# Attention transposes in a graph kernel: 128x128 transposes on TensorE replaced by 32x32 block transposes on VectorE and a round trip through DRAM

## The chip, the cores and the metric

The kernel runs on one core of one Trainium2 chip. Its time is the device time of one execution in microseconds (us). The kernel before takes 3298.03 us, the median of three runs between 3296.64 and 3298.12 us. The engines are called as in the profile: PE is TensorE (PEld its weight loads), DVE VectorE, ACT ScalarE, POOL GpSimd; SP is the engine whose queue issues all the DMAs of this kernel.

## The reference

There are 128 graphs of 128 nodes with 256 features each, all in float32. Three layers of graph attention are followed by a gated graph network (GRU) of three steps. Each layer works on the normalized, rectified input and adds its result to it:

```python
h = jnp.maximum(_layernorm(x, axis=-1), 0.0)
x = x + gnn(h, adj, W, a)          # three attention layers
# one attention layer, per graph
Wh = h @ W
e = leaky_relu((Wh @ a1)[:, None] + (Wh @ a2)[None, :], 0.2)
att = softmax(where(adj > 0, e, -9e15), axis=-1)
out = elu(att @ Wh)                # the third layer multiplies by a node mask before elu
# the gated layer, three steps
aggr = A.T @ (h @ weight[i])
r, z = sigmoid(..), sigmoid(..);  n = tanh(i_n + r * h_n)
h = (1 - z) * n + z * h
```

A matrix product on TensorE sums over the partitions of both operands. `h @ W` therefore needs h with its features on the partitions, and `att @ Wh` needs att with its columns on the partitions. Both lie the other way round when they are computed, node by partition, so each attention layer transposes h (two blocks of 128x128 per graph) and att (one block per graph), and the gated network needs the transpose of its first h as well.

## The kernel before

The 128 graphs are worked on in 32 groups of G = 4. For each group there are two programs. `gat(g)` (lines 276 to 295) loads x and adj, derives two masks from adj (`cap`, `am`), runs three attention layers and then the normalization for the gated network. `gru(g)` (lines 297 to 393) runs three steps of the gated network and stores the result. They are written down in the order gat(0), gat(1), gru(0), gat(2), gru(1), gat(3), and so on (lines 401 to 407). The Tile framework then orders the instructions by itself: it plays the program through ahead of time, and among the instructions whose operands it holds to be ready an engine takes the one that was written down first. The result is one fixed order per engine, and on the chip an engine that waits for an operand holds up everything behind it in its own order. So an instruction of gat(g+1) goes ahead of gru(g) and behind gru(g-1), and gru(g) fills what gat(g+1) leaves free.

A tile with a tag has as many buffers as its pool says, and the tiles of one tag take them in the order in which they are written down. The pools `gw` and `grp` have two buffers (the tags `x3` and `am` three). PSUM's eight banks are dealt out by line 62: three to attention (`gat`), four to the GRU's gates (`gru`), one to the GRU's transposes and aggregations (`tr`).

One attention layer (lines 196 to 272) goes as follows.

- `normed` (line 162): DVE takes mean and variance of each row (`st`, `mv`, lines 167 and 168), POOL turns the variance into 1/sqrt (`ve`, `rs`, lines 170 and 172), DVE writes the normalized rows `xn` (line 175).
- `relu_T` (line 181): eight PE transposes of 128x128 into two PSUM banks (`hTp`, line 187), which ACT (line 191) and DVE (line 193) rectify into `hT`.
- `whp` (line 207): PE multiplies hT by W, to which two columns W@a1 and W@a2 are appended; ACT copies each result to `wh` (line 211).
- `e` (line 216) spreads the second score along the rows with a PE transpose of a broadcast column; DVE adds the first score, applies the mask and the leaky slope and takes the row maximum (lines 222 to 228); ACT takes the exponential and its row sums (line 232); DVE inverts the sums (line 236); POOL scales the rows (`pe`, line 239) and prepares x - 1 (`xm`, line 244).
- `atp` (line 248): four PE transposes of att, which DVE copies to `at` (line 250).
- `hp` (line 256): PE multiplies at by wh; ACT and DVE compute elu and add x (lines 262 to 268), which gives the x of the next layer, `xo`.

After the third layer, `normed` and `relu_T` run a fourth time (lines 290 to 293): hT is then the first h of the GRU with features on partitions, and POOL rectifies xn into `hn`, the same with nodes on partitions. In the GRU the transposes `hnp` (line 308) turn later h back to nodes on partitions, `agp` (line 334) multiplies by the adjacency, and the gate products go through `mm` (line 317).

All DMAs are issued by SP: loads of x and adj at lines 69 and 71, the store of the result at line 392.

Of the kernel before, what the change touches and what calls it, by code (L numbers as in the profile page):

```python
# [8 lines left out]
FT = mybir.dt.float32  # L9
# [12 lines left out]
def kernel(  # L22
# [23 lines left out]

    nc = tc.nc
# [14 lines left out]
    BANKS = {"gat": 3, "gru": 4, "tr": 1}  # L62
# [95 lines left out]
    setup.close()  # L158
    rw = ctx.enter_context(tc.tile_pool(name="rw", bufs=2))


    def normed(xt, name):
# [3 lines left out]
        for b in range(G):  # L166
            nc.vector.bn_stats(st[:, b, :], xt[:, b, :])  # L167
            nc.vector.bn_aggr(mv[:, b, :], st[:, b, :])
        ve = gw.tile([P, G], FT, tag="ve", name=f"ve_{name}")
# [3 lines left out]
        xn = gw.tile([P, G, D], FT, tag="xn", name=f"xn_{name}")  # L173
        for b in range(G):
            nc.vector.tensor_scalar(  # L175
                xn[:, b, :], xt[:, b, :], mv[:, b, 0:1], rs[:, b : b + 1],
                op0=OP.subtract, op1=OP.mult,
            )
        return xn

    def relu_T(xn, pool, tag, name):

        hT = pool.tile([P, KD, T], FT, tag=tag, name=f"hT_{name}")
        for k in range(KD):
            ps = bank("gat", f"hTp_{name}_{k}")
            for b in range(G):
                nc.tensor.transpose(  # L187
                    ps[:, b * P : (b + 1) * P], xn[:, b, k * P : (k + 1) * P], ident
                )
            if k % 2 == 0:  # L190
                nc.scalar.activation(hT[:, k, :], ps, AF.Relu)  # L191
            else:
                nc.vector.tensor_scalar_max(hT[:, k, :], ps, 0.0)
        return hT

    def attention(g, l, xt, cap):

        name = f"{g}_{l}"
        xn = normed(xt, name)
        hT = relu_T(xn, gw, "hT", name)  # L200
# [3 lines left out]
        for c in range(G):  # L204
            ps = bank("gat", f"whp_{name}_{c}")
            for k in range(KD):
                nc.tensor.matmul(  # L207
                    ps[:, :E], hT[:, k, c * P : (c + 1) * P], W[l][:, k, :],
                    start=(k == 0), stop=(k == KD - 1),
                )  # L210
            nc.scalar.copy(wh[:, c, :], ps[:, :E])  # L211
# [17 lines left out]
        pe = gw.tile([P, G, N], FT, tag="pe", name=f"pe_{name}")  # L229
        sm = gw.tile([P, G], FT, tag="sm", name=f"sm_{name}")  # L230
        for b in range(G):
            nc.scalar.activation(
                pe[:, b, :], em[:, b, :], AF.Exp, bias=nmx[:, b : b + 1], accum_out=sm[:, b : b + 1]
# [3 lines left out]
        if l == 2:  # L237
            nc.vector.tensor_mul(ri, ri, nmT[:, g * G : (g + 1) * G])
        nc.gpsimd.tensor_tensor(  # L239
            pe, pe, ri.rearrange("p (g o) -> p g o", o=1).to_broadcast([P, G, N]), op=OP.mult  # L240
        )

        xm = gw.tile([P, G, D], FT, tag="xm", name=f"xm_{name}")
        nc.gpsimd.tensor_scalar(xm, xt, 1.0, -1.0, op0=OP.mult, op1=OP.add)
        yield
        atp = bank("gat", f"atp_{name}")
        for b in range(G):
            nc.tensor.transpose(atp[:, b * P : (b + 1) * P], pe[:, b, :], ident)
        at = gw.tile([P, T], FT, tag="at", name=f"at_{name}")
        nc.vector.tensor_copy(at, atp)  # L250
        xo = grp.tile([P, G, D], FT, tag=f"x{l + 1}", name=f"xo_{name}", bufs=3 if l == 2 else 2)
        for j in range(G // 2):
            hp = bank("gat", f"hp_{name}_{j}")
            for b in range(2):
                c = 2 * j + b
                nc.tensor.matmul(  # L256
                    hp[:, b * D : (b + 1) * D], at[:, c * P : (c + 1) * P], wh[:, c, :D],
# [5 lines left out]
            u = gw.tile([P, T], FT, tag="u", name=f"u_{name}_{j}")  # L263
            nc.vector.scalar_tensor_tensor(  # L264
                u, hp, 0.0, xm[:, 2 * j : 2 * j + 2, :].rearrange("p b d -> p (b d)"),
                op0=OP.max, op1=OP.add,
            )
            nc.vector.scalar_tensor_tensor(  # L268
# [174 lines left out]
```

## Time and profile before

| | before |
|---|---|
| median of three runs | 3298.03 us |
| the profiled execution: its time, its span | 3297.82 us, 3296.0 us |
| granted TensorE clock, mean | 0.992 |
| PE busy | 3089.3 us, 94% |
| DVE busy | 1889.7 us, 57% |
| ACT busy | 1076.1 us, 33% |
| POOL busy | 461.8 us, 14% |
| DMA share of 16 engines | 4.5% in the one queue that carries the kernel's own data |

The span is the time from the first to the last instruction. Busy time counts an instruction from start to end, and a matmul overlaps the next one, so a row of matmuls is better measured by the distance between their starts; the chain view gives that distance, since it lists each instruction only up to the start of what follows it. "The chain" is the sequence of work that ended last, followed back from the last instruction to whatever released it. "To landing" is the time from the issue of a DMA to the moment at which its completion is signalled. A float32 product appears as two matmul instructions.

### The profile page before, as it was taken

The page shows a single profiled execution, that of the slowest core. Times are in us where ns is not written, and L with a number is a line of the kernel's source. Part 1 is how long each engine was busy: PE and PEld are TensorE (multiplying, and loading weights), DVE is VectorE, ACT ScalarE, POOL GpSimd, SP SyncE. Part 2 cuts the span into 40 slices and gives each one's busy share as a digit, 9 for nine tenths or more (in the row PEclk, how much of TensorE's full clock was granted, in tenths as well). Part 3 has the DMA queues.
Part 4 walks back from the last instruction along what each step waited for, and adds up shares of the span by engine and source line. Part 5 has one row for each costly group of instructions (what it writes and reads, how often), then busy time and mean ns, then how long its engine had stood idle before and what let it go on. Part 6 is the DMA issues. An engine that isn't in the chain of part 4 may idle for free.

```text
span 3296.0 us, 30815 instructions
## 1 busy us (share of the span) xinstructions
PE 3089.3 (94%) x11093; PEld 1743.6 (53%) x11093; DVE 1889.7 (57%) x4216; ACT 1076.1 (33%) x2369; POOL 461.8 (14%) x486
## 2 busy tenths in 40 slices
PE   5799999999999999999999999999999999999999
PEld 3455555555555555555555555555555555555554
DVE  4555655555655555655556555556555556555553
ACT  1233333333333333333333333333333333333332
POOL 0111111111111111111111111111111111111110
PEclk8899999999999999999999999999999999999999
DMA  2000000000000000000000000000000000000000
GB/s 81 10 16 17 10 7 17 17 16 10 13 10 17 17 17 10 7 17 17 16 17 10 7 17 16 17 10 16 7 17 17 17 10 7 16 13 7 7 1 13
DMA packets 56186, 47.93 MB, mean 15 GB/s; under 512 B 3296, under 2 KB 55648, under 8 KB 56032
## 3 DMA queue, kind: packets, MB, share of 16 engines
q1 hardware_dynamic: 56032, 45.95, 4.5%
q8 instruction: 87, 1.43, 0.2%
q14 instruction: 67, 0.55, 0.1%
HBM read 29.17 MB, written 16.78 MB: 14 GB/s over the span
## 4 chain that ended last, share of the span: by engine, by line
PE 60%; DVE 22%; POOL 10%; ACT 5%; issue 2%; DMA 0%; SPq 0%; ACTq 0%; POOLq 0%; DVEq 0%
PE r L317 11%; PE whp L207 11%; PE z L317 10%; PE nn L317 6%; PE ni L317 5%; PE hTp L187 5%; POOL rs L172 4%; DVE u L264 4%; DVE xo L268 4%; DVE st L167 3%; PE agp L334 3%; POOL pe L239 3%; PE hp L256 3%; DVE xn L175 3%; PE hnp L308 2%
## 5 line engine op out<-in xcount | busy, mean ns | idle before, releaser
L317 PE MATMUL r<-ag,wc 128*128 128x512 f32 x768 | 377.8, 597 | 0.0
L317 PE MATMUL z<-ag,wc 128*128 128x512 f32 x768 | 371.0, 592 | 0.0
L207 PE MATMUL whp<-w,hT 128*128 128x258 f32 x1536 | 368.9, 389 | 0.3 <-ACT hT L191 0.2
L317 PE MATMUL ni<-ag,wc 128*128 128x512 f32 x768 | 366.1, 592 | 0.0
L239 POOL TENSOR_TENSOR pe<-pe,ri 128x512 f32<-128x512 f32 x96 | 99.9, 1040 | 1893.4 <-PE agp L334 988.9
L363 ACT ACTIVATE r<-r,brz 128x512 f32<-128x512 f32 x192 | 132.0, 687 | 602.0 <-PE r L317 602.0
L207 PEld LDWEIGHTS whp<-w,hT 128*128 128x128 f32 x1536 | 283.7, 191 | 82.0 <-ACT hT L191 16.2
L222 DVE SCALAR_TENSOR_TENSOR em<-e,wh,cap 128x128 f32<-128x128 f32 x384 | 108.1, 344 | 380.4 <-PE e L216 380.4
L358 ACT ACTIVATE wn<-nn,bh 128x512 f32<-128x512 f32 x192 | 132.0, 687 | 532.7 <-PE nn L317 532.7
L365 DVE SCALAR_TENSOR_TENSOR n<-r,wn 128x512 f32<-128x512 f32 x192 | 131.8, 687 | 303.4 <-ACT r L363 303.3
L187 PE MATMUL hTp<-ident,xn 128*128 128x128 f32 x1024 | 185.9, 292 | 107.2 <-DVE xn L175 107.2
L317 PE MATMUL nn<-h,whh 128*128 128x512 f32 x512 | 261.8, 593 | 0.0
L317 PE MATMUL z<-h,whh 128*128 128x512 f32 x512 | 261.5, 592 | 0.0
L317 PE MATMUL r<-h,whh 128*128 128x512 f32 x512 | 261.3, 592 | 0.0
L334 PEld LDWEIGHTS agp<-am,hn 128*128 128x128 f32 x1536 | 205.6, 192 | 99.1 <-issue 62.6
L317 PEld LDWEIGHTS z<-ag,wc 128*128 128x128 f32 x768 | 143.5, 190 | 168.9 <-issue 168.9
L211 ACT COPY wh<-whp 128x258 f32<-128x258 f32 x384 | 143.9, 375 | 262.2 <-PE whp L207 262.2
L317 PEld LDWEIGHTS ni<-ag,wc 128*128 128x128 f32 x768 | 143.3, 190 | 155.3 <-issue 153.6
L187 PEld LDWEIGHTS hTp<-ident,xn 128*128 128x128 f32 x1024 | 118.0, 142 | 202.8 <-PE z L317 91.4
L334 PE MATMUL agp<-am,hn 128*128 128x128 f32 x1536 | 215.6, 277 | 1.7 <-POOL hn L293 1.6
L175 DVE TENSOR_SCALAR xn<-xo,mv,rs 128x256 f32<-128x256 f32 x384 | 132.6, 408 | 142.9 <-POOL rs L172 142.9
L317 PEld LDWEIGHTS r<-ag,wc 128*128 128x128 f32 x768 | 133.1, 190 | 132.9 <-issue 91.7
(80 smaller groups left out, 4425.8 us busy)
## 6 DMA issues: line engine op xcount, KB each, us to landing
x<-in_x_dram SPq DMA_DIRECT2D x32, 512.0 KB, 3.9
out_dram<-o SPq DMA_DIRECT2D x32, 512.0 KB, 2.9
adj<-in_adj_dram SPq DMA_DIRECT2D x32, 256.0 KB, 2.7
w<-in_L_gnn_W_dram SPq DMA_DIRECT2D x3, 256.0 KB, 5.8
ab<-in_L_gnn_a_dram SPq DMA_DIRECT2D x3, 256.0 KB, 5.5
whh_ld<-in_L_gnn_w_hh_dram SPq DMA_DIRECT2D x1, 768.0 KB, 8.4
wih_ld<-in_L_gnn_w_ih_dram SPq DMA_DIRECT2D x1, 768.0 KB, 6.6
gt_ld<-in_L_gnn_weight_dram SPq DMA_DIRECT2D x3, 256.0 KB, 3.0
```

Source lines behind the costliest of these rows:

```text
L172: nc.gpsimd.tensor_tensor(rs, ve, mhalf, op=OP.pow)
L175: nc.vector.tensor_scalar(xn[:, b, :], xt[:, b, :], mv[:, b, 0:1], rs[:, b : b + 1], op0=OP.subtract, op1=OP.mult,)
L187: nc.tensor.transpose(ps[:, b * P : (b + 1) * P], xn[:, b, k * P : (k + 1) * P], ident)
L207: nc.tensor.matmul(ps[:, :E], hT[:, k, c * P : (c + 1) * P], W[l][:, k, :], start=(k == 0), stop=(k == KD - 1),)
L211: nc.scalar.copy(wh[:, c, :], ps[:, :E])
L239: nc.gpsimd.tensor_tensor(pe, pe, ri.rearrange("p (g o) -> p g o", o=1).to_broadcast([P, G, N]), op=OP.mult)
L264: nc.vector.scalar_tensor_tensor(u, hp, 0.0, xm[:, 2 * j : 2 * j + 2, :].rearrange("p b d -> p (b d)"), op0=OP.max, op1=OP.add,)
L268: nc.vector.scalar_tensor_tensor(xo[:, 2 * j : 2 * j + 2, :].rearrange("p b d -> p (b d)"), t, 1.0, u, op0=OP.min, op1=OP.add,)
L317: nc.tensor.matmul(ps, w[:, k, c * P : (c + 1) * P], v[k], start=start, stop=stop)
L334: nc.tensor.matmul(ps[:, b * P : (b + 1) * P], hn[k][b], am[:, b, :], start=True, stop=True)
L358: nc.scalar.activation(wn, nn, AF.Identity, bias=bh[:, cn : cn + 1])
L363: nc.scalar.activation(r, pr, AF.Tanh, bias=brz[:, cr : cr + 1], scale=0.5)
```

## The change

The transposes `hTp` and `atp` leave TensorE. DVE's `transpose` turns every 32x32 block of its operand in place of its own, so a 128x128 matrix comes out as a 4x4 grid of turned blocks that still stand in their old places. Moving block (q, j) to place (j, q) means moving it to other partitions. That is done by DMA: `exchange` stores the turned tile to a DRAM tile in one DMA and reads it back with four, each of which fills 32 partitions from four places in DRAM. All five are issued by SP, and the four reads wait for the store.

Around it:

- `stats` takes the place of `normed`. xn is now relu(x - mean) by ACT, without the factor rs, which is positive and is applied later, when ACT copies `whp` to `wh`. DVE negates the mean (`nm`).
- `turned` makes DVE's block transposes (two of 512 elements per partition for xn, one for att) and calls `exchange`. The elements are written interleaved by graph and feature half, so that each row in DRAM is contiguous; hT and at are therefore read by the matmuls with a step of 8 and of 4 elements between neighbouring columns, where the columns lay side by side before.
- The exponential is written over its input `em`, and the scaling by the inverted sums moves from POOL to DVE.
- POOL writes x - 1 directly into `xo`, and the elu steps work in place there; the tiles `xm`, `u` and `pe` are gone.
- For the GRU's first h, ACT computes `hn` with both mean and rs; DVE turns its two halves and each goes through its own exchange. The result stays ordered by block, and the first GRU step reads it through a rearranged pattern (`like`).
- PSUM banks: attention has two in place of three, the GRU's transposes and aggregations two in place of one.

The transposes `e`, `hnp` and those of the weights at the start stay on TensorE.

```diff
-    BANKS = {"gat": 3, "gru": 4, "tr": 1}
+    BANKS = {"gat": 2, "gru": 4, "tr": 2}
+    Q = P // 32
...
+    dram = ctx.enter_context(tc.tile_pool(name="dram", bufs=3, space=bass.MemoryType.DRAM))
...
+        nm = gw.tile([P, G], FT, tag="nm", name=f"nm_{name}")
+        nc.vector.tensor_scalar(nm, mv[:, :, 0], -1.0, None, op0=OP.mult)
         ve = gw.tile([P, G], FT, tag="ve", name=f"ve_{name}")
         nc.gpsimd.tensor_scalar(ve, mv[:, :, 1], EPS, None, op0=OP.add)
         rs = gw.tile([P, G], FT, tag="rs", name=f"rs_{name}")
         nc.gpsimd.tensor_tensor(rs, ve, mhalf, op=OP.pow)
+        return nm, rs
+
+    def exchange(tr, out, name):
+        d = dram.tile([Q, 32, Q, tr.shape[2]], FT, tag=f"d{tr.shape[2]}", name=f"d_{name}")
+        nc.sync.dma_start(d.rearrange("q r j f -> (q r) j f"), tr)
+        for j in range(Q):
+            nc.sync.dma_start(
+                out[j * 32 : (j + 1) * 32], d[:, :, j, :].rearrange("q r f -> r q f")
+            )
+
+    def turned(v, out, name):
+        m = v.shape[2] // P
+        tr = gw.tile([P, Q, 32, G, m], FT, tag=f"tr{m}", name=f"tr_{name}")
+        for k in range(m):
+            nc.vector.transpose(
+                tr[:, :, :, :, k].rearrange("p j c b -> p b j c"),
+                v[:, :, k * P : (k + 1) * P].rearrange("p b (j r) -> p b j r", j=Q),
+            )
+        exchange(
+            tr.rearrange("p j c b k -> p j (c b k)"),
+            out.rearrange("p (q c) f -> p q (c f)", q=Q), name,
+        )
...
         for b in range(G):
-            nc.vector.tensor_scalar(
-                xn[:, b, :], xt[:, b, :], mv[:, b, 0:1], rs[:, b : b + 1],
-                op0=OP.subtract, op1=OP.mult,
-            )
...
-        hT = relu_T(xn, gw, "hT", name)
+            nc.scalar.activation(xn[:, b, :], xt[:, b, :], AF.Relu, bias=nm[:, b : b + 1])
+        hT = gw.tile([P, N, G * KD], FT, tag="hT", name=f"hT_{name}")
+        turned(xn, hT, name)
...
-                    ps[:, :E], hT[:, k, c * P : (c + 1) * P], W[l][:, k, :],
+                    ps[:, :E], hT[:, :, c * KD + k], W[l][:, k, :],
...
-            nc.scalar.copy(wh[:, c, :], ps[:, :E])
+            nc.scalar.activation(wh[:, c, :], ps[:, :E], AF.Copy, scale=rs[:, c : c + 1])
...
-        nc.gpsimd.tensor_tensor(
-            pe, pe, ri.rearrange("p (g o) -> p g o", o=1).to_broadcast([P, G, N]), op=OP.mult
+        nc.vector.tensor_tensor(
+            em, em, ri.rearrange("p (g o) -> p g o", o=1).to_broadcast([P, G, N]), op=OP.mult
         )
...
+        nc.gpsimd.tensor_scalar(xo, xt, 1.0, -1.0, op0=OP.mult, op1=OP.add)
+        at = gw.tile([P, N, G], FT, tag="at", name=f"at_{name}")
+        turned(em, at, f"{name}_a")
         yield
-        atp = bank("gat", f"atp_{name}")
-        for b in range(G):
-            nc.tensor.transpose(atp[:, b * P : (b + 1) * P], pe[:, b, :], ident)
-        at = gw.tile([P, T], FT, tag="at", name=f"at_{name}")
-        nc.vector.tensor_copy(at, atp)
...
-                    hp[:, b * D : (b + 1) * D], at[:, c * P : (c + 1) * P], wh[:, c, :D],
+                    hp[:, b * D : (b + 1) * D], at[:, :, c], wh[:, c, :D],
...
-        xn = normed(xt, f"{g}_3")
-        hT = relu_T(xn, grp, "h0", f"{g}_3")
+        nm, rs = stats(xt, f"{g}_3")
+        nc.vector.tensor_mul(nm, nm, rs)
         hn = grp.tile([P, G, D], FT, tag="hn0", name=f"hn_{g}_0")
-        nc.gpsimd.tensor_scalar(hn, xn, 0.0, None, op0=OP.max)
+        for b in range(G):
+            nc.scalar.activation(
+                hn[:, b, :], xt[:, b, :], AF.Relu, bias=nm[:, b : b + 1], scale=rs[:, b : b + 1]
+            )
+        hT = []
+        for k in range(KD):
+            tr = gw.tile([P, Q, G, 32], FT, tag="tr3", name=f"tr_{g}_3_{k}")
+            nc.vector.transpose(
+                tr.rearrange("p j b c -> p b j c"),
+                hn[:, :, k * P : (k + 1) * P].rearrange("p b (j r) -> p b j r", j=Q),
+            )
+            t = grp.tile([P, Q, G, 32], FT, tag=f"h0{k}", name=f"h_{g}_0_{k}")
+            exchange(
+                tr.rearrange("p j b c -> p j (b c)"), t.rearrange("p q b c -> p q (b c)"),
+                f"{g}_3_{k}",
+            )
+            hT.append(t.rearrange("p q b c -> p b q c"))
```

## The prediction

> **What bounds the kernel now.** I read the page first, then the stages, the chain through one layer, the order of DVE and PE around the change of groups, and the DMA issues. The page shows PE as the fullest engine, and the stages (columns: stretch, its length, busy time and instructions of PE, PEld, DVE, ACT, POOL, clock, DMA share, GB/s) show a steady state that repeats: 95.36 us of PE in every 100.
>
> ```profile
> PE 3089.3 (94%) x11093; PEld 1743.6 (53%) x11093; DVE 1889.7 (57%) x4216; ACT 1076.1 (33%) x2369; POOL 461.8 (14%) x486
> 1520.00:1620.00 100.00, 95.36 (x348) 53.79 (x347) 58.47 (x131) 33.69 (x75) 14.41 (x15) 1.00 0.04 14
> 1620.00:1720.00 100.00, 95.36 (x348) 53.78 (x347) 58.48 (x131) 33.69 (x75) 14.41 (x15) 1.00 0.05 14
> ```
>
> The first GRU product starts at 120.1 us and that of the last group at 3217.7, so one group takes (3217.7 - 120.1)/31 = 99.9 us. The profiled time is then 120.1 + 31 x 99.9 + 80.1 (last group and what lies around the span) = 3297.8, against a median of 3298.03.
>
> The attention of a group is a chain of its own beside PE. One layer in the chain view (start, us, what):
>
> ```profile
> 1542.10 1.05 POOL rs L172
> ...
> 1543.18 0.42 DVE xn L175
> ...
> 1543.73 1.64 PE hTp L187 x8
> 1545.38 0.86 PE nn L317 x2
> 1546.24 3.62 PE whp L207 x16
> ...
> 1556.18 0.10 DVE ri L236
> ...
> 1556.41 1.05 POOL pe L239
> ...
> 1557.50 0.66 PE atp L248 x4
> ...
> 1559.45 0.88 PE hp L256 x4
> ...
> 1566.53 1.05 POOL rs L172
> ```
>
> From rs to rs a layer takes 24.4 us. Two stretches hold the change: from the last mv (1541.7) over rs, xn and hTp to whp, 4.5 us; and from ri (1556.3) over pe and atp to hp, 3.2 us.
>
> The last view is the order on DVE and PE (start, us, engine, line, operation):
>
> ```profile
> 1589.57 0.39 DVE L167 BATCH_NORM_STATS2 st<-xo 128x6 f32<-128x256 f32 x1
> 1589.88 0.17 DVE L168 BATCH_NORM_AGGREGATE mv<-st 128x2 f32<-128x6 f32 x1
> 1589.96 0.40 DVE L167 BATCH_NORM_STATS2 st<-x 128x6 f32<-128x256 f32 x1
> ...
> 1599.54 1.38 DVE L175 TENSOR_SCALAR xn<-x,mv,rs 128x256 f32<-128x256 f32 x4 [1.47 <-POOL rs L172]
> ...
> 1619.98 1.04 PE L187 MATMUL hTp<-ident,xn 128*128 128x128 f32 x8
> ```
>
> The next group's first statistics (st<-x) come directly behind the fourth statistics of this group, although x was loaded long before; the same is seen at the start of the kernel (112.7 and 113.1). Two buffers of the tag st, taken in written order, say why. So the attention of two groups does not overlap: one period cannot be shorter than three layers plus the 2.2 us of the fourth statistics. That is 3 x 24.4 + 2.2 = 75.4 us now, and the finished xn waits from 1600.9 to 1619.98 for PE, which is still in the previous GRU. PE bounds the period, and the attention chain has slack below it.
>
> **The change, part by part.** *What PE loses.* Eight hTp take 0.87 us by the distance of starts, so 32 of them 3.5 us and 12 atp at the same distance 1.3 us per group; PE's waits for xn (107.2 us in all) and for pe (53.5) are 5.0 us per group. PE alone would then allow 99.9 - 4.8 = 95.1, or with all the waits gone 90.1.
>
> *What the chain gains.* The exchange is in no row; its legs are. These are issue to landing, columns KB and us:
>
> ```profile
> x<-in_x_dram SPq DMA_DIRECT2D x32, 512.0 KB, 3.9
> out_dram<-o SPq DMA_DIRECT2D x32, 512.0 KB, 2.9
> adj<-in_adj_dram SPq DMA_DIRECT2D x32, 256.0 KB, 2.7
> ```
>
> The store of hT is 512 KB, as out: 2.9 us (bounds 2.2, the price taken below for half the bytes, and 3.9, x). Its four reads of 128 KB carry together what x carries, in the same 1 KB pieces: 3.9 (bounds 2.7, and 5.0 when the last of four issues, each 0.37 to 0.38 us on SP, starts 1.1 us late). For att the store is 256 KB: 2.2, between half of out (1.45) and adj (2.7); the reads 3.3, as the last of four starts 1.1 late and lands 2.2 later (bounds 2.2 and 3.8).
>
> First stretch after: nm 0.2 (128x6 on DVE: 0.17); four relu on ACT at 0.42, between the copy of 128x258 (0.375) and half again of the 512-wide n (0.719), 1.7; two DVE transposes at 0.69, as the 512-wide at copy (0.692), 1.4; four hand-overs of 0.1; store 2.9, reads 3.9. Sum 10.5 against 4.5: **+6.0**. The DVE transpose has no row: bounds 0.42 (cap, 512 wide) and 1.39 (half of POOL's 2.779 for 1024, the slowest plain rate here); 0.69 is DVE's usual price. The rs path on POOL (1.3 us) leaves the chain, because rs is now wanted only at the copy of whp; the exchange hides it, and without that cover it costs 1.4.
> Second stretch after: product on DVE 0.69, transpose 0.69, hand-overs 0.3, store 2.2, reads 3.3. Sum 7.2 against 3.2: **+4.0**.
>
> A layer is then 24.4 + 10.0 = 34.4, and the period 3 x 34.4 + 2.2 = **105.4**. The chain passes PE's 90 to 95 and becomes the bound; PE is what now waits.
>
> *The start.* Layer 0 of group 0 has its xn at 12.5 while PE is in the weights until 40.7, so its first exchange is hidden (cost 6.0 if not); +4.0 for its second, +20.0 for the next two layers. Fourth stage, before: mv at 113.1 to the GRU at 120.1, 7.0. After: rs 1.9, nm times rs 0.2, four hn 1.7, two transposes 1.3, hand-overs 0.3, store 2.2, reads 3.3, four more issues of the second exchange 1.5: 12.4, so +5.4. The first GRU starts at 149.5. The last GRU runs without attention: 80.1 as before.
>
> Sum: 149.5 + 31 x 105.4 + 80.1 = 3497.
>
> *What lies beside it, at nothing.* SP issues 8 exchanges x 5 = 40 more DMAs per group, 15 us of 105; behind its waiting reads stand the loads of x and adj, wanted a period later, and the store of out, wanted by nobody. DVE loses xn, one hT and at (11.3 us) and gains 11 transposes, nm and the product (10.6); ACT gains 16 x 0.42 - 4 x 0.6 = 4.3 us on 33.7; POOL loses 5.9 of 14.4. All have room in 105. x - 1 on POOL (1.05) lies beside the exchange of att. Two attention banks: a whp result is copied (0.38) while the next is computed (0.9); uncovered, 0.4 per product. Two tr banks take at most the waits for ag (19.1 + 54.8 us in all, 2.3 per group) off PE, which does not bind. The first GRU step's rearranged reads are hidden by the 13 us that PE has spare (105.4 less 92.6, the middle of its 90.1 to 95.1).
>
> *A rule against the change.* Row first: a whp weight load takes 190 ns (at most 338 in this trace), and whp products start 226 ns apart (3.62/16), so a load fits behind its predecessor.
> The Trainium skill, SBUF — State Buffer, Specifications, gives SBUF 16-byte lines and asks for two hits in each for full bandwidth; hT is now read one value every 32 bytes, at one every 16. If that doubled the load to 380 ns, my estimate from this page is 154 ns per product, some 2.5 us per layer in whp and 1.3 in hp, and 3850 us in all; no row here shows such a read.
> The Trainium skill, VectorE: DVE Perf Modes, The three transpose paths, gives 311 ns for a 128x128 transpose on DVE; four of them are 1.24 us as an estimate, and the sum by it 3650; no transpose of DVE is in this trace.
>
> **The rivals.**
> *PE stays the bound, faster.* If both exchanges of a layer land sooner, the chain falls below PE. The point is 31 x period = 3297.8 - 149.5 - 80.1, a period of 99.0, or +7.9 per layer in place of +10.0. With every leg at its lowest bound (2.2, 2.7, 1.45, 2.2: 3.75 less) the layer gains 6.3, and with transposes at 0.42 5.5: the chain is then 92 and PE bounds at about 92.6. The start comes some 8 earlier, 142, total 142 + 31 x 92.6 + 80.1 = 3093. For it: DMA engines are 4.5% busy and four reads run side by side. Against: each landing here has a floor (adj is half of x and takes 2.7 of 3.9). An overlap of two groups' attention would end here too; the order of st speaks against it.
> *SP's queue.* The fourth stage's ten DMAs stand ahead of the next group's first exchange, whose store waits for their store and eight issues: 2.2 + 3.0 = 5.2 per period, 3658. For it: one queue; against: the order is planned by readiness.
> *Strided operands.* With loads at 338 ns (whp 16 x 0.112, hp 0.5) and transposes at 1.39 (3 x 0.7) a layer gains 4.4 more: period 118.6, 3906.
>
> **How the numbers follow.** Chances: the forecast 0.62 (of it 0.02 at a period near 99.0, which is no change, and 0.01 just below), PE bound 0.18, SP's queue 0.12, strided operands 0.08. The forecast's own range is 3340 to 3720 (+8.3 to +12.3 per layer, the reads at their bounds). The range 3090 to 3780 reaches half of the PE case and leaves the strided one out. About 0.2% is what a measurement of this kernel can tell from no change: faster 0.19, same 0.02, slower 0.79.
>
> **What would show it.** Right: periods of the first GRU product near 105 us; PE busy below 90% with gaps ended by the DMAs of hT and at; a chain with DMA, SP, DVE and ACT in every layer and few GRU products; st<-x still behind the fourth st; a store near 2.9 us and reads near 3.9. Wrong: a period near 93 with PE above 95%; landings below 2 us; st<-x of the next group before the third layer ends; PEld of whp far above 190 ns; DVE's transposes far from 0.69 us. The prediction fails most easily by the landing times, which enter six times in each period.

## The result and the profile after

The changed kernel takes 4150.03 us, the median of four runs between 4148.20 and 4153.94, against 3297.34 us for the kernel before. The ratio is 1.2588, with a 95% interval of 1.2566 to 1.2609. The direction was forecast; the size was not: 3497 was expected, and 4150 lies far above the upper end of the range, 3780.

The page of the changed kernel, engines and granted clock in 40 slices:

```profile
PE 3171.6 (76%) x9685; PEld 1885.7 (45%) x9685; DVE 2007.6 (48%) x4088; ACT 1274.5 (31%) x2753; POOL 263.1 (6%) x358
PEclk7788988888988888988889888889888898888898
```

PE has 1408 instructions fewer than before and is busy for 82 us more: its clock is no longer granted in full, 0.848 in the mean against 0.992, and whp, which now loads with a step, takes 4.01 us per layer at full clock in place of 3.78. The first GRU product starts at 154.7 us and that of the last group at 4071.2, so a period is 126.3 us where the forecast had 105.4 and the kernel before 99.9.

One period in stretches (the same columns as for the stages before): the last 38 us before the next GRU starts, in two parts, and then the GRU beside layers 0 and 1, in two parts.

```profile
1504.80:1530.50 25.70, 10.57 (x28) 7.98 (x28) 8.56 (x20) 4.75 (x14) 0.00 (x0) 0.63 0.15 51
1530.50:1542.80 12.30, 3.98 (x16) 3.69 (x16) 7.32 (x23) 3.67 (x8) 2.53 (x4) 0.50 0.42 124
1542.80:1577.00 34.20, 34.14 (x100) 19.49 (x101) 12.68 (x22) 11.13 (x24) 0.00 (x0) 0.94 0.15 48
1577.00:1617.60 40.60, 40.58 (x132) 23.14 (x131) 24.57 (x46) 15.88 (x33) 3.36 (x4) 1.00 0.13 40
```

There are two regimes. While the GRU runs, PE works without a gap (34.14 of 34.20, 40.58 of 40.60). When it is done, layer 2 and the fourth statistics are alone: PE is busy for 14.6 of 38 us, and its clock is granted at 0.63 and 0.50 of full speed.

Layer 2 in the timeline (start, us, engine, line, operation), the rows that answer to rs, hTp, whp, pe, atp and hp of before:

```profile
1494.10 1.71 ACT L210 ACTIVATE xn<-xo,nm 128x256 f32<-128x256 f32 x4 [0.96 <-DVE nm L173]
...
1495.84 2.04 DVE L194 STREAM_TRANSPOSE tr<-xn 128x512 f32<-128x512 f32 x2 [1.77 <-ACT xn L210]
...
1497.91 0.34 SPq L183 DMA_DIRECT2D d<-tr  x1
...
1500.58 1.73 SPq L185 DMA_DIRECT2D hT<-d  x4
...
1504.89 6.15 PE L219 MATMUL whp<-w,hT 128*128 128x258 f32 x16 [0.99 <-DMA hT<-d]
...
1517.60 1.08 DVE L194 STREAM_TRANSPOSE tr_a<-em 128x512 f32<-128x512 f32 x1
1518.71 0.34 SPq L183 DMA_DIRECT2D d_a<-tr_a  x1
1520.79 1.75 SPq L185 DMA_DIRECT2D at<-d_a  x4
...
1524.20 3.77 PE L263 MATMUL hp<-wh,at 128*128 128x256 f32 x8 [12.27 <-DMA at<-d_a]
```

From the issue of the store to whp are 7.0 us, from that of the second store to hp 5.5. The landings (KB, median us to landing):

```profile
d<-tr SPq DMA_DIRECT2D x96, 512.0 KB, 2.6
hT<-d SPq DMA_DIRECT2D x384, 128.0 KB, 2.9
d_a<-tr_a SPq DMA_DIRECT2D x96, 256.0 KB, 2.0
at<-d_a SPq DMA_DIRECT2D x384, 64.0 KB, 2.0
```

Layer 0 of the next group, the same rows, is far longer:

```profile
1535.45 1.69 ACT L210 ACTIVATE xn<-x,nm 128x256 f32<-128x256 f32 x4
...
1537.38 2.01 DVE L194 STREAM_TRANSPOSE tr<-xn 128x512 f32<-128x512 f32 x2
1538.38 3.64 SPq L185 DMA_DIRECT2D h<-d  x8
...
1542.11 0.38 SPq L183 DMA_DIRECT2D d<-tr  x1
...
1545.26 1.73 SPq L185 DMA_DIRECT2D hT<-d  x4
...
1555.37 4.01 PE L219 MATMUL whp<-w,hT 128*128 128x258 f32 x16
```

The turned rows are there at 1539.4, but SP first issues eight reads of h for the GRU, which wait for their stores, and issues this store at 1542.11. The reads of hT are issued at 1545.26, and whp starts 10.1 us later, with no wait on a DMA in its row: PE is in the GRU's products. Layer 2, where PE is free, needs 4.3 us for the same step.

From the first statistics of a layer to those of the next, layer 0 takes 47.6 us, layer 1 39.4, layer 2 37.0, where the forecast had 34.4 for each. The link between the groups is as forecast (2.0 us): the next group's statistics still come directly behind the fourth of this one.

```profile
1528.52 0.43 DVE L170 BATCH_NORM_STATS2 st<-xo 128x6 f32<-128x256 f32 x1
...
1530.54 0.39 DVE L170 BATCH_NORM_STATS2 st<-x 128x6 f32<-128x256 f32 x1
```

### The profile page after: what moved, and what is told of

The parts are those of the page before. It is cut to its first block, busy times and chain, and to the rows that moved or that the text cites. A ratio compares the mean times of both kernels' runs of the same rounds, so it can differ in the third digit from the quotient of the medians.

```text
span 4149.5 us, 31019 instructions
## 1 busy us (share of the span) xinstructions
PE 3171.6 (76%) x9685; PEld 1885.7 (45%) x9685; DVE 2007.6 (48%) x4088; ACT 1274.5 (31%) x2753; POOL 263.1 (6%) x358
## 4 chain that ended last, share of the span: by engine, by line
PE 56%; issue 29%; DVE 5%; DMA 5%; POOL 2%; ACT 2%; SPq 1%; POOLq 0%; DVEq 0%; ACTq 0%
PE r L338 14%; PE z L338 13%; PE nn L338 8%; PE ni L338 7%; PE whp L219 6%; PE agp L355 3%; DMA h<-d 2%; PE hp L263 2%; POOL rs L177 2%; DMA d<-tr 2%; PE hnp L325 1%; ACT hn L295 1%; DVE xo L271 1%; DVE xo L272 1%; SPq L185 1%
## 5 line engine op out<-in xcount | busy, mean ns | idle before, releaser
L263 PE MATMUL hp<-wh,at 128*128 128x256 f32 x768 | 256.4, 490 | 417.9 <-DMA at<-d_a 417.8
L338 PE MATMUL nn<-h,whh 128*128 128x512 f32 x768 | 425.8, 638 | 160.5 <-DMA h<-d 160.5
L338 PE MATMUL r<-h,whh 128*128 128x512 f32 x768 | 419.2, 629 | 0.0
L263 PEld LDWEIGHTS hp<-wh,at 128*128 128x128 f32 x768 | 209.9, 328 | 453.4 <-issue 295.6
L338 PE MATMUL z<-h,whh 128*128 128x512 f32 x768 | 399.6, 602 | 0.0
L223 ACT ACTIVATE wh<-whp,rs 128x258 f32<-128x258 f32 x384 | 183.0, 477 | 462.1 <-PE whp L219 462.1
L338 PEld LDWEIGHTS nn<-h,whh 128*128 128x128 f32 x768 | 142.3, 204 | 266.8 <-DMA h<-d 142.8
L194 DVE STREAM_TRANSPOSE tr<-xn 128x512 f32<-128x512 f32 x192 | 195.2, 1092 | 111.9 <-ACT xn L210 111.9
L338 PEld LDWEIGHTS z<-h,whh 128*128 128x128 f32 x768 | 153.7, 200 | 199.6 <-issue 171.3
L391 ACT ACTIVATE n<-n,bi 128x512 f32<-128x512 f32 x192 | 138.6, 722 | 336.1 <-DVE n L390 336.1
```

The source lines that it names most:

```text
L194: nc.vector.transpose(tr[:, :, :, :, k].rearrange("p j c b -> p b j c"), v[:, :, k * P : (k + 1) * P].rearrange("p b (j r) -> p b j r", j=Q),)
L223: nc.scalar.activation(wh[:, c, :], ps[:, :E], AF.Copy, scale=rs[:, c : c + 1])
L263: nc.tensor.matmul(hp[:, b * D : (b + 1) * D], at[:, :, c], wh[:, c, :D], start=True, stop=True,)
L338: nc.tensor.matmul(like(ps, v[k]), w[:, k, c * P : (c + 1) * P], v[k], start=start, stop=stop)
L391: nc.scalar.activation(n, n, AF.Tanh, bias=bi[:, cn : cn + 1])
```

## The experiments

Times stand against the kernel before on the same chip (3297.7 to 3299.3 us). Periods are taken as above, from the first GRU product of the first group to that of the last, divided by 31; layer lengths come from the statistics in DVE's timeline, for one group near 1500 us.

**Two groups' attention allowed to overlap.**

```diff
-        st = gw.tile([P, G, 6], FT, tag="st", name=f"st_{name}")
+        st = gw.tile([P, G, 6], FT, tag=f"st_{half[0]}", name=f"st_{name}")
...
-    BANKS = {"gat": 2, "gru": 4, "tr": 2}
+    BANKS = {"gat0": 1, "gat1": 1, "gru": 4, "tr": 2}
```

`half[0]` is g % 2, and all tags of the pool `gw`, the DRAM tiles and attention's banks are split so.

> The changed kernel with the attention tiles, the DRAM tiles and the attention banks of PSUM split by even and odd group: a set for each, one buffer per tag in place of two shared by all, one PSUM bank each in place of two shared. The memory stays about the same, but the attention of the next group no longer has to wait for the tiles of this one in written order. Chain theory (the 126 us of a period are the attention chain of one group, and the next can't start before its end): two chains run side by side, the period falls to what PE allows, 93 to 100 us, and the time to 3050 to 3300 us. Rival (PE itself became slower, through strided weight loads and a lower clock): the period stays above 115 us and the time above 3800.

Measured: 3650.21 us, ratio 1.1066 (1.105 to 1.1083). Two groups repeat every 221.7 us, 110.9 for each. So 500 us of the 853 lost are hidden once two groups' attention may overlap. It doesn't reach PE's bound: with one bank for each half, whp now waits 95.4 us in all for ACT's copy `wh`, and hp 104.0 for the reads of at.

**The exchange left out.** The matmuls read the turned tile itself, so the blocks stay in their old places.

```diff
-        exchange(
-            tr.rearrange("p j c b k -> p j (c b k)"),
-            out.rearrange("p (q c) f -> p q (c f)", q=Q), name,
-        )
+        return tr.rearrange("p j c b k -> p (j c) (b k)")
```

> The changed kernel without the round trip through DRAM: the matmuls read the turned tile directly, so the 32x32 blocks stay in their old places and the output is not the reference's; everything else stays, the strided reads too. Chain theory: a layer loses 7.0 + 5.5 us of exchange, the attention chain falls from 126 to about 85 us per period and PE becomes the bound: 93 to 98 us per period, 3050 to 3200 us in all. Rival (strided operands and the clock carry the loss): a loss remains, above 3500 us.

Measured: 3160.3 us, 0.9581 (0.9566 to 0.9595). PE is busy for 94% of the span at a clock of 0.989 and the period is 95.6. All of the loss, and more, hangs on the round trip.

**Neighbouring elements in place of strided ones, the DMAs as they are.** DVE writes its blocks side by side and whp and hp load neighbouring columns, so the blocks of the operands are mixed up.

```diff
-                tr[:, :, :, :, k].rearrange("p j c b -> p b j c"),
+                flat[:, k * T : (k + 1) * T].rearrange("p (b j c) -> p b j c", b=G, j=Q),
...
-                    ps[:, :E], hT[:, :, c * KD + k], W[l][:, k, :],
+                    ps[:, :E], hT.rearrange("p n f -> p (n f)")[:, (c * KD + k) * P : (c * KD + k + 1) * P], W[l][:, k, :],
```

> The changed kernel with the same DMAs, but DVE's transposes of xn and att write side by side and the matmuls of whp and hp read 128 neighbouring columns as weights; the columns are then the wrong ones, so the output is not the reference's. Strided-operand theory: weight loads fall from 334 to 190 ns, transposes from 1.09 to 0.69 us, and 1.2 us of transposes per layer plus up to 2.3 us of whp and hp leave the chain: the period falls by 4 to 10 us, 3840 to 4030 us. Rival (strides are hidden): within 20 us of 4150.

Measured: 4073.86 us, 1.2355 (1.2334 to 1.2375): 76 us, between the two expectations. DVE's transpose falls from 1092 to 687 ns. The stride is a cost, but only 9% of the loss.

**The fourth stage's ten DMAs on ACT's queue.**

```diff
-    def exchange(tr, out, name):
+    def exchange(tr, out, name, q=nc.sync):
...
-                f"{g}_3_{k}",
+                f"{g}_3_{k}", nc.scalar,
```

> The changed kernel with the ten DMAs of the fourth stage issued by ACT in place of SP, so that the first exchange of the next group no longer stands behind them. SP-queue theory: that store is issued 2.7 us sooner (1542.1 to 1539.4) and the period falls by 2.5 to 4 us, 4020 to 4075 us. Rival (PE's fixed order decides: the whp of layer 0 stood behind GRU products until 1555.5 although its operand landed near 1550): no change, 4130 to 4170. A third outcome: ACT's own queue is held up by its waits for the stores, slower than 4170.

Measured: 4162.17 us, 1.2615 (1.2596 to 1.2633), no gain. Layer 0 became 2.8 us shorter, but layer 1 took 42.5 us in place of 39.4. SP's queue is a delay at its place and not the bound.

**One kind of transpose back on PE at a time.** In the first kernel att, in the second the rows for hT and for the GRU, in the third all are turned by PE again (`turned_pe`: four transposes into a bank and a copy), and in the fourth only the GRU's h is exchanged. A layer's operand that PE turns is also loaded from neighbouring columns again, so these runs take back an exchange together with DVE's transposes and the strided loads that go with it.

```diff
-        turned(em, at, f"{name}_a")
-        yield
+        yield
+        turned_pe(em, at, f"{name}_a")
```
```diff
-        turned(xn, hT, name)
+        turned_pe(xn, hT, name)
```

> The changed kernel with one exchange taken back: att is transposed on PE again (four products into an attention bank, one copy by DVE to side-by-side columns), while the transposes of the normalized rows, in the layers and for the GRU, keep the exchange. Theory (each exchange costs its own latency on the chain, the att exchange 6.25 us per layer as read in layer 2 of the profile): three layers give back some 19 us of the period of 126.1, so a period near 107 and a time of 3500 to 3620 us. Rival (the lateness of hp and whp in PE's fixed order multiplies the latency, so that removing one of two exchanges frees far more than its own latency): a period near the 95 to 100 that PE allows, under 3400 us. Rival (the fixed share of PE's cold clock and the fourth stage decide, the att exchange is hidden): over 3950 us.

Measured: 3817.98 us, 1.1576 (1.1559 to 1.1593). Period 116.0, layers 41.1, 36.5 and 36.4 us. None of the three ranges held: taking one exchange of each layer away gives back some 10 us per group, not 19. Here too whp comes late, in layer 1 at 1583.80, 9.0 us after the reads were issued.

> The changed kernel with the other exchange taken back: the normalized rows are transposed on PE again in the three layers and for the GRU (copied from PSUM by ACT and DVE), while att keeps DVE's transpose and the exchange. Theory (latencies add): the first stretches of the layers, which came out at +17.5, +9.9 and +6.1 us over the 4.5 of before, go back to about 4.5, so 33 us of 126.1 return and a period of 95 to 100 with PE near its bound, 3150 to 3350 us. Rival (the same lateness arises at hp instead, since PE's planned order again puts GRU products ahead): a period of 105 to 112, 3450 to 3680 us.

Measured: 3226.99 us, 0.9785 (0.9769 to 0.9801). Period 97.2, layers 33.5, 31.1 and 30.7 (layer 0 is 31.9 in every other group). The chain is back near PE's bound, as the theory had it. The two exchanges are not symmetric: att's alone costs 71 us over having none (3156), the other 662, both together 994. The first 71 are small, as I read it, because the chain had slack under PE's bound.

> The changed kernel with all transposes back on PE and no exchange at all: statistics, ACT's rectified rows, the factor rs in the copy of whp, the in-place exponential and elu and the banks 2, 4, 2 stay as changed. Theory (the other edits are worth little or something good): with no round trip PE bounds, the period is the 95.1 of the version without a round trip plus up to 4.8 us of PE's transposes, 3160 to 3300 us. Rival (two banks for attention or the work moved to ACT and DVE cost as much as the exchange hides): over 3310 us, which would mean that part of the loss of the change comes from its other edits.

Measured: 3156.31 us, 0.9571 (0.9556 to 0.9585): faster than both kernels, with no exchange at all. The change's other edits gain 141 us, and with the strided operands the transposes that it took off PE are worth nothing on top (3160.3 without the round trip). What PE waited for in this kernel (us in all, times, longest):

```profile
PE tp L208 <- ACT hn L308: 38.8, 32, 6.3
PE tp_a L208 <- DVE em L263: 21.8, 35, 5.8
...
PE tp L208 <- ACT xn L223: 8.9, 2, 4.5
```

Before, the waits for xn, pe and ag in this view were 107.2, 53.5 and 19.1 us, together 180; now they are 70.

> The changed kernel with only the fourth stage's two exchanges, for the first h of the GRU; hT and at of the three layers are transposed on PE as in rest_alone (3156.31 us). Theory (the exchange costs time only where the chain of attention has no slack; with the layers short the chain has some 20 us of slack per group, and the two exchanges are hidden): 3150 to 3200 us. Rival (the GRU's start waits for its h in every group and PE idles for it): 3250 to 3500 us.

Measured: 3160.07 us, 0.9582 (0.9568 to 0.9596). With short layers the GRU's two exchanges are hidden, as expected. An exchange costs what the chain has no slack for.

**Where the 141 us come from: banks or the other edits.** One line each way.

```diff
-    BANKS = {"gat": 3, "gru": 4, "tr": 1}
+    BANKS = {"gat": 2, "gru": 4, "tr": 2}
```

> The kernel before with one line changed: PSUM banks 2, 4, 2 for attention, the GRU's gates and the GRU's transposes, in place of 3, 4, 1. Theory (the 141 us that the edits without the exchange gain come mostly from the second bank for the GRU's transposes): 3150 to 3220 us. Rival (they come from the work moved off the way between the statistics and the first transposes, and PE's waits for xn and pe stay here): 3260 to 3310 us. Rival (attention needs its third bank when its transposes go through it): over 3310 us.

> The version of rest_alone, all transposes on PE and no exchange, with the banks of before, 3, 4, 1. Theory (the second bank for the GRU's transposes makes most of the gain): 3250 to 3300 us. Rival (the statistics, ACT's rows and the late rs make it): 3140 to 3190 us.

Measured: the kernel before with the new banks 3289.91 us, 0.9976 (0.9966 to 0.9986); the version of `rest_alone` with the old banks 3155.69, 0.957 (0.9556 to 0.9585). Both lie in the range of the rival that the banks don't matter: they are worth 8 us and nothing. The gain comes from the other edits together. That it is the shorter way from the statistics to xn and from ri to the transposes is my reading, from the 110 us by which PE's waits fell; the edits were not run one by one.

**Attention alone.** The GRU is left out of both kernels: gru(g) adds and stores what attention made.

```diff
-        h = h0
...
         o = rw.tile([P, G, D], FT, tag="o", name=f"o_{g}")
-        for k in range(KD):
-            ps = node_major(STEPS, k)
...
+        nc.vector.tensor_add(o, xt, hn0)
         nc.sync.dma_start(out[g * G : (g + 1) * G].rearrange("b n d -> n b d"), o)
         yield
```

> The changed kernel without the gated network: gru(g) only adds the third layer's x and the rectified rows and stores them; the attention, all exchanges and the setup are unchanged. It leaves out the GRU, so its time is that of the chain of attention with no other work on PE. Theory (the chain is 37 us per layer as in layer 2 of the profile, where PE is nearly free of the GRU, and the other 15 us of the 126.1 come from waiting behind GRU products and behind the fourth stage): a period of 108 to 118 us, 3500 to 3800 us in all. Rival (PE's order is no part of the cost and the chain alone is as long): a period of 122 to 128, over 3900 us. Rival (the cold clock and the exchange add less when alone): under 105, the 34.4 per layer of the forecast.

> The kernel before without the gated network: gru(g) only adds the third layer's x and the rectified rows and stores them. It leaves out the GRU, as attention_alone does for the changed kernel, so the difference of the two (attention_alone took 3883.97 us) is the price of the change in the chain of attention with nothing else on PE. Theory (the exchange itself costs about the 10 us per layer of the forecast, and what the changed kernel lost beyond that comes from PE's lower clock and from its planned order): 2800 to 3050 us, a difference of 26 to 34 us per group. Rival (the exchange itself is dearer than priced): under 2750 us. Rival (most of the chain of attention_alone is the low clock, not the exchange): over 3150 us.

Measured: 3883.97 us for the changed kernel and 2728.73 for the one before. The first lies in none of its ranges, above the theory's; the second is the rival's outcome, an exchange dearer than priced. In the mean over the groups the periods, from statistics to statistics, are 120.1 and 83.9 us. Layer 1 of the changed one (from st over the exchanges to whp, to hp, to the next st), and then the same layer of the one before:

```profile
1508.89 0.43 DVE L170 BATCH_NORM_STATS2 st<-xo 128x6 f32<-128x256 f32 x1
...
1513.87 2.02 DVE L194 STREAM_TRANSPOSE tr<-xn 128x512 f32<-128x512 f32 x2 [1.77 <-ACT xn L210]
...
1515.92 0.34 SPq L183 DMA_DIRECT2D d<-tr  x1
...
1518.62 1.73 SPq L185 DMA_DIRECT2D hT<-d  x4
...
1523.40 5.63 PE L219 MATMUL whp<-w,hT 128*128 128x258 f32 x16 [14.98 <-DMA hT<-d]
...
1536.29 0.34 SPq L183 DMA_DIRECT2D d_a<-tr_a  x1
...
1538.35 1.73 SPq L185 DMA_DIRECT2D at<-d_a  x4
...
1541.76 3.77 PE L263 MATMUL hp<-wh,at 128*128 128x256 f32 x8 [11.85 <-DMA at<-d_a]
...
1546.08 0.43 DVE L170 BATCH_NORM_STATS2 st<-xo 128x6 f32<-128x256 f32 x1
```
```profile
1486.27 0.42 DVE L167 BATCH_NORM_STATS2 st<-xo 128x6 f32<-128x256 f32 x1
...
1492.78 5.76 PE L207 MATMUL whp<-w,hT 128*128 128x258 f32 x16
...
1507.04 3.70 PE L256 MATMUL hp<-wh,at 128*128 128x256 f32 x8 [0.78 <-DVE at L250]
...
1512.08 0.42 DVE L167 BATCH_NORM_STATS2 st<-xo 128x6 f32<-128x256 f32 x1
```

With nothing else on PE, this layer takes 37.2 us against 25.8: 14.5 against 6.5 to whp (+8.0), 18.4 against 14.3 to hp (+4.1), 4.3 against 5.0 behind it. All three layers with their link cost 36.2 us more per group (120.1 less 83.9).

Layer 0 of the kernel before, alone, is longer than its layer 1:

```profile
1539.97 0.40 DVE L167 BATCH_NORM_STATS2 st<-x 128x6 f32<-128x256 f32 x1
...
1543.39 2.78 POOL L293 TENSOR_SCALAR hn<-xn 128x1024 f32<-128x1024 f32 x1 [1.51 <-DVE xn L175]
...
1546.45 1.88 POOL L172 TENSOR_TENSOR rs<-ve,mhalf 128x4 f32<-128x4 f32 x1
...
1551.34 5.50 PE L207 MATMUL whp<-w,hT 128*128 128x258 f32 x16 [0.47 <-ACT hT L191]
...
1570.23 0.42 DVE L167 BATCH_NORM_STATS2 st<-xo 128x6 f32<-128x256 f32 x1
```

From st to whp are 11.4 us here and 6.5 in layer 1: POOL first makes hn of the group before, and rs comes behind it. Up to 0.8 us of this may belong to the experiment itself: rs takes 1.88 us here and 1.04 in layer 1, and the added sum runs on DVE meanwhile.

**PE's order and the fourth stage.** The GRU's products are made to stand behind whp where the planned order had them ahead; `behind` gives them a place in PE's order and no wait, and `at` counts half steps of the GRU.

```diff
+                at = 2 * i + c % KD + (w is not whh) / 2
+                with behind(g + 1, 1 if at >= 3.5 else 0 if at >= 0.5 else -1):
```

> The changed kernel with PE's order altered and nothing else: in layers 0 and 1 of the next group whp goes ahead of six GRU products that the planned order puts before it. Theory (hT has landed and whp stands behind these products: in layer 0 its reads are issued at 1545.26 and whp starts at 1555.37, in layer 1 1588.22 and 1595.41, against 4.3 us from issue to start in layer 2): layer 0 shortens by some 5 us, layer 1 by 2 to 3, the period goes from 126.1 to 117 to 120, 3860 to 3960 us. Rival (hT lands later there than in layer 2, and PE would now wait for it): the period moves by less than 2 us, over 4080 us.

Measured: 4132.47 us, 1.2524 (1.2503 to 1.2544). The time is the rival's, the mechanism isn't: whp of layer 0 starts 4.7 us after its reads are issued and doesn't wait, so hT had landed. Its rows:

```profile
1542.48 1.73 SPq L185 DMA_DIRECT2D hT<-d  x4
...
1547.16 4.11 PE L221 MATMUL whp<-w,hT 128*128 128x258 f32 x16
```

Layer 0 fell from 47.6 to 43.9 us. But layer 1 rose from 39.4 to 41.8 and layer 2 from 37.0 to 38.4, and the period went from 126.3 to 125.9 only.

In the next kernel the GRU's h is turned by PE, and only the layers exchange.

```diff
-            exchange(
-                tr.rearrange("p j b c -> p j (b c)"), t.rearrange("p q b c -> p q (b c)"),
-                f"{g}_3_{k}",
-            )
+        turned_pe(hn, hT, f"{g}_3")
```

> The changed kernel with the fourth stage's two exchanges taken back: hn is transposed by PE for the GRU, and hT and at of the three layers keep the exchange. Theory (the fourth stage's transposes on DVE and its ten DMAs on SP stand ahead of layer 0's own, 1.5 and 2.7 us, and its late h holds up the GRU that layer 0's whp then stands behind): layer 0 shortens from 47.6 us by 4 to 9, 3850 to 4030 us. Rival (layer 0 is long because of PE's order alone, which stays): over 4080 us. Rival (the fourth stage carries most of the loss, since the GRU can't start without it): under 3700 us.

Measured: 4143.51 us, 1.256 (1.2542 to 1.2579). The same again: layer 0 43.9, layer 1 42.0, layer 2 38.6, period 126.2. What layer 0 gave up, the others took.

Then whp before GRU products in all three layers, alone and together with the edit of `layers_only`:

```diff
+                at = 2 * i + c % KD + (k / 4 if w is whh else 0.5)
+                with behind(g + 1, sum(at >= v for v in (0.5, 3.25, 5.5)) - 1):
```

> The changed kernel with PE's order altered as in whp_first, but in all three layers: six GRU products stand behind whp in layer 0, nine in layer 1, and the last six of the GRU behind whp of layer 2. Theory (lateness of whp at every layer, 5.8 and 2.9 us, in layer 2 the wait for the GRU's end): layer 1 near 38 us in place of 41.8 in whp_first, the period 118 to 121, 3890 to 3990 us. Rival (PE's gapless stretch and the tail set the period): within 40 us of 4150.

> attention_order with the fourth stage's exchanges taken back as in layers_only, hn turned on PE for the GRU. Theory (both delays are real and each was hidden behind the other): layer 0 near 39 us, the period 113 to 117, 3730 to 3870 us. Rival (PE's gapless stretch and the tail set the period): over 4000 us.

Measured: 4132.85 us, 1.2532 (1.2511 to 1.2552), period 125.6; and 4045.86 us, 1.2267 (1.2249 to 1.2285), period 123.1. The first is the rival's outcome, and the second lies in the rival's range as well, at its lower end: the order alone gives 17 us, the fourth stage alone 7, the two together 104. So each of the two delays was hidden behind the other, but together they hold 3.2 us of a period and not the 9 to 13 expected. Layers 1 and 2 stay at 39.9 and 39.4.

**The strides where PE binds.** The version without a round trip, with the edit of `contiguous`.

> no_round_trip (3160.3 us) with whp and hp loading neighbouring columns and DVE writing its blocks side by side; no exchange, so blocks stand in the wrong places and the output is not the reference's. Theory (PE binds there, and the loads of 334 ns at a step of 32 bytes in place of 190 cost what the removed transposes saved): whp's 16 products take 3.62 us in place of 4.0 and hp loses some 0.2, 2 to 3 us per group, 3070 to 3110 us. Rival (the loads are hidden and another wait took the gain): within 20 us of 3160.

Measured: 3050.08 us, 0.9245 (0.9231 to 0.9258), 110 us below `no_round_trip` and more than expected; period 92.2. In the two, the products of whp, their weight loads and the products of hp, with what ended the waits before them; then the weight loads in the changed kernel:

```profile
L216 PE MATMUL whp<-w,tr 128*128 128x258 f32 x1536 | 437.2, 428 | 37.1 <-DVE tr L194 27.1 <-issue 6.9
...
L216 PEld LDWEIGHTS whp<-w,tr 128*128 128x128 f32 x1536 | 386.9, 332 | 111.0 <-DVE tr L194 59.9 <-PE nn L330 32.7 <-issue 14.8
...
L260 PE MATMUL hp<-wh,tr_a 128*128 128x256 f32 x768 | 212.4, 421 | 41.1 <-DVE tr_a L194 41.1
```
```profile
L217 PE MATMUL whp<-w,tr 128*128 128x258 f32 x1536 | 368.2, 389 | 16.6 <-DVE tr L195 6.9 <-issue 6.5
...
L217 PEld LDWEIGHTS whp<-w,tr 128*128 128x128 f32 x1536 | 276.2, 192 | 113.3 <-issue 35.6 <-DVE tr L195 28.5 <-ACT wh L221 15.4
...
L261 PE MATMUL hp<-wh,tr_a 128*128 128x256 f32 x768 | 193.4, 395 | 18.6 <-DVE tr_a L195 18.5
```
```profile
L219 PEld LDWEIGHTS whp<-w,hT 128*128 128x128 f32 x1536 | 412.1, 334 | 123.2 <-issue 86.5
```

Transposes off PE, with their copies, are worth 106 us here (3156 to 3050), and the strides take all of it back, on two engines that this edit doesn't separate. PE's busy time falls by 69 us in all (2975.2 to 2906.0), as its products load faster. Its waits for DVE's transposes, which took 1.10 us each and now take 0.69 to 0.71, fall by 43 (27.1 + 41.1 to 6.9 + 18.5), although DVE is busy for only 61% of the span.

## Why the prediction was wrong

**What bounds the kernel after: right.** The chain of attention passes PE. The link of 2.0 us, the order of st and the waits of hp on at<-d_a (417.8 us in all) are as the prediction said, and `overlap` shows what the serial order is worth.

**The exchange's price: nearly right.** Store and reads were priced at 2.9 + 3.9 and 2.2 + 3.3. In the chain alone they take 2.70 + 4.78 and 2.06 + 3.41. The second stretch came out at +4.1 for +4.0.

**The first stretch: mis-sized, +8.0 for +6.0.** Two transposes take 2.02 us and not 1.4, the reads 0.9 more than priced, and DVE's elu step that now stands between the statistics adds 0.7. The three layers together cost 36.2 us per group where 30.0 was said: +6.2 per period. The price of 0.69 for a transpose was right for blocks written side by side (687 ns in `contiguous`); written interleaved it is 1092. The Trainium skill, VectorE: DVE Perf Modes, The three transpose paths, gives its 311 ns for a 128x128 transpose in bf16, which the prediction didn't say. The estimate of 1.24 us for four blocks, worked out from it, lies above both of the times that float32 took here.

**"3 x 24.4 + 2.2 = 75.4 us now": the step that failed first.** I read one layer from rs to rs and took it three times. With the GRU gone the chain of before repeats in 83.9 us, 8.5 more. Layer 0 is 30.0 us in the mean and not 24.4, because the fourth statistics, xn, hn and hT of the group before stand in its way on DVE, POOL and PE (up to 0.8 us of it may be the experiment's own); in the trace of before this lay under layer 0's wait for PE and I didn't look for it. The other two layers are 0.9 and 2.1 longer, at the low clock that PE has alone (0.67, where the 16 products of whp take 5.76 us). The prediction has no term for the clock.

**"All have room in 105": the step that failed second.** The busy shares leave room on average, but the period has a stretch of some 83 us in which PE has no gap and one of 43 in which it has little to do. Beside the GRU the changed kernel's layers cost 126.3 - 120.1 = 6.2 us more than alone. The three terms make up the whole miss per period: 8.5 + 6.2 + 6.2 = 20.9, and 31 times that is 648 of 653 us. They add up by the way they are defined, as steps from 75.4 over 83.9 and 120.1 to 126.3, so the sum is no test of them. The split between the first and the last is not sharp, since the clock differs between a kernel with and without the GRU.

**The last 6.2: only partly settled.** Late whp is real (10.1 us after the reads in layer 0, 7.2 in layer 1, 4.3 in layer 2), and so are the eight reads of h ahead of layer 0's store. But four runs that took one such delay away left the period between 125.6 and 126.6. From the first GRU product to the end of layer 1 are 74.7 us in the changed kernel, 73.9 with ACT's queue and 73.4 with whp first. My reading is that in a stretch without a gap an earlier whp only moves GRU products behind it, and with them the GRU's work on DVE and ACT that layer 1 then meets. That is argued, not shown; both delays taken away gave 3.2 us, and the rest stays open.

**The start and the end: close.** The first GRU product came at 154.7 for 149.5, and the last group's 78 us answer to 80.1.

**The rivals.** PE staying the bound was wrong, though its price was good: 92.6 us per period was said, 92.2 came out without strides and 95.6 with them. SP's queue is refuted as a bound by `act_queue`. Strided operands, at 3906 the nearest number, were not the reason: the loads did go to 334 ns, near the 338 of that case, but the whole effect here is 76 us and not 409. The Trainium skill, SBUF — State Buffer, Specifications, pointed the right way: its lines of 16 bytes led to an estimate of 380 ns for a load of 190, and 334 was measured. What the estimate missed is that loads and products overlap: a layer's whp took 4.01 us at full clock, 250 ns for each product with a load of 334, and not 3.62 + 2.5.

## What to carry to other kernels

A latency that is added to a serial chain is hidden only up to that chain's slack, and the slack must be read from the whole chain, its first and last stage too, not from the layer that is easiest to see; running the chain alone, with the other work left out, measures it in one run, though at the clock that the emptier engine then has. Busy shares averaged over a period don't show that it has a full and an empty part, and here a delay taken away in the full part came back elsewhere. Look at what else comes with a change: here the edits around the transposes gain 4.3% by themselves, and the part that gave the change its name costs all of that and 26% of the old time besides.

## What the runs showed of the hardware

- PE's granted clock was lower where PE waited: 0.63 and 0.50 in the stretches in which it was busy for 41% and 32%, 0.94 and 1.00 in those without a gap, and 0.593 in the mean with attention alone. The same 16 products of whp took 6.15 us in layer 2 and 4.01 in layer 0, behind GRU products. A wait on PE's path therefore cost more than its own length here.
- A weight load of 128x128 float32 takes 192 ns from neighbouring columns (`free_unstrided`, whp), 332 at a step of 32 bytes and 326 at 16 bytes (`no_round_trip`, whp and hp), at mean clocks of 0.979 and 0.989.
- A 32x32 block transpose on DVE of 512 float32 per partition takes 687 to 711 ns in the mean where the elements of a block row are written side by side (`contiguous`), and 1092 to 1105 where they are written 32 or 16 bytes apart (the changed kernel, `no_round_trip`).
- Landing follows the size only in part here: a store took 2.0 us with 256 KB and 2.6 with 512 KB, each of four reads 2.0 us with 64 KB and 2.9 with 128 KB. Each of the eight reads of h, 64 KB as well, took 3.0.
